# A transformer block in one kernel: token loads of the QKV stages written fifteen steps earlier, and GpSimd's low parts pinned to written order

## The chip, the cores and the metric

The kernel runs on one core of one Trainium2 chip. The metric is the device time of one execution in microseconds (us), as the median of several runs. A profiled execution gives one trace more, and all durations in this text come from such traces.

## What is computed

The reference is a transformer block whose normalised inputs and whose branches are modulated by a condition. There are 2 batch rows of 2048 tokens, 512 features, 16 heads of 32 features and a hidden layer of 2048.

```python
mod = silu(condition) @ Wada + bada
sh_a, sc_a, gt_a, sh_m, sc_m, gt_m = jnp.split(mod, 6, axis=1)
xn = _layernorm(x, g1, be1)
xm = xn * (1.0 + sc_a[:, None, :]) + sh_a[:, None, :]
x = x + gt_a[:, None, :] * _attention(xm, Wqkv, Wproj, bproj)   # causal
xn = _layernorm(x, g2, be2)
xm = xn * (1.0 + sc_m[:, None, :]) + sh_m[:, None, :]
h = gelu(xm @ W1 + b1)
x = x + gt_m[:, None, :] * (h @ W2 + b2)
```

All of it is in float32. The change lies in the part that makes queries, keys and values out of the modulated tokens.

## The kernel before, in words

**Stages.** For batch row 0 and then for row 1 the kernel makes queries, keys and values (the QKV stage) and runs attention. The projection of row 0 stands ahead of row 1's QKV stage, that of row 1 ahead of the MLP, which then runs over all tokens. In the trace the QKV stage of row 0 ends at about 205 us and that of row 1 lies between about 775 and 955 us.

**A QKV stage.** The class `Qkv` (L898) takes a batch row's 2048 tokens in four groups g = 0 to 3 of 512 tokens, that is four tiles of 128 tokens. For each group it runs six units u: units 0 to 3 make the queries and keys of one chunk f of 128 features (four heads), units 4 and 5 the values. A unit (`unit`, L1002) has seven products on half-sized blocks that are summed on three PSUM banks a, b and c, a Strassen-like scheme. Bank a is accumulated on four times and bank b twice; between two of these ScalarE or VectorE copies or adds what the bank holds into an SBUF tile (`first`, `last`, `direct`). The seventh product of a unit is run as third step of the unit after it (`late`, L1197). So a group has 42 steps n, seven a unit, and after each step `tick` (L1145) issues other work of that step. The text writes (g, n) for step n of group g. The first group of a stage has 41 ticks, since no late product precedes its units.

**What a tick does for the next group.** Group g + 1's tokens are loaded at n = 3 (`load_x`, L915, four DMAs of 256 KB on SyncE's queue, into a tile tag `x` with four buffers, so that one group's tokens fill it). Their statistics come at n = 10 to 13 (L218 on VectorE, not pinned), the scaling at n = 15 and 25 (L964 on ScalarE, in place), the transposes on TensorE with the modulation behind them at n = 18 and 28 (`norm`, L970, L214). In row 1's stage the tokens of group 1 are loaded by the projection ahead of it. From n = 7 of group 1 on, each tick also computes some attention scores of the first units of that row (`row.score`): a matmul into one of two banks `s` (L482), and a row maximum of it on VectorE (L498, L504). How many is planned by `count` (L534) from `cum`, a sum of costs by unit (L288: w + 190 for a maximum over w columns, w + 250 where the mask is added): over groups 2 and 3 the plan rises evenly from `cum[0]` to `cum[2]`, and unit 2 comes only when unit 1 is spent.

**High and low parts.** Each result of queries and keys is kept as two tiles: `hi` (L1064, a copy on ScalarE rounded to fp32r) and `lo`, the difference (L1066). For groups 0 and 1 VectorE makes the difference, for groups 2 and 3 GpSimd. Chunk f's queries are split at n = 7f + 5, its keys in the late product at n = 7f + 9. Both tiles are then stored by SyncE (`stored`, L1025, L1031), and the stored heads are read back for the scores (L335, L360) a few ticks after chunk 0's keys. Tiles `hi` have three buffers, tiles `lo` five in row 0 and six in row 1. A unit takes two `lo` tiles, one for queries, one for keys, and both get their first data from bank a and bank b.

**Weight pieces of the MLP.** `Pieces` (L1205) makes sums of blocks of W1 and W2 beside the QKV stages: at a planned tick SyncE loads a piece into idle buffers (L1230, L1239), some ticks later GpSimd begins its sums (L1251), one a tick, or two while more than 12 are waiting, and then stores it (L1267, L1271). A piece in row 0's stage has 4 sums and a store, the last one in row 1's stage 16 sums and a store; that one is loaded at piece tick 74 and begun at tick 80 (L1578).

**What sets the order.** Each engine executes its instructions in the order in which they were put into its queue. The framework chooses that order: it runs the program through a model, and gives each engine at each time the first instruction in written order that the model takes to be ready. An instruction wrapped in `mm` (L204) or `act` (L208) is pinned: it comes behind the instruction written just before it on its engine. All matmuls and the sums of pieces are pinned; DMAs on SyncE, ScalarE's copies, VectorE's statistics and both differences of L1066 aren't.

Of the kernel before, what the change touches and what calls it, by code (L numbers as in the profile page):

```python
# [8 lines left out]
F32 = mybir.dt.float32  # L9
# [3 lines left out]
ALU = mybir.AluOpType  # L13
# [14 lines left out]
def dit_block_kernel(  # L28
# [46 lines left out]
    NG = T // MT  # L75
# [128 lines left out]
    def mm(*args, **kw):  # L204

        return tc.keep_in_program_order(nc.tensor.matmul(*args, **kw))  # L206

    def act(ins):  # L208

        return tc.keep_in_program_order(ins)  # L210
# [687 lines left out]
    class Qkv:  # L898
# [142 lines left out]
        def keys_and_queries(self, g, f, hp):  # L1041

            ops = self.operands(g)
            los = [self.lo_tile(hp) for _ in range(2)]

            def part(i, j):
                return los[i].bitcast(F32)[:, j * HALF_T : (j + 1) * HALF_T]

            def product(ps, n, new):
                for k in range(HK):  # L1050
                    mm(
                        ps, self.w[:, n, k, f * P : (f + 1) * P], ops[n][:, k],
                        start=new and k == 0, stop=k == HK - 1,
                        skip_group_check=not new,
                    )

            def first(ps, i, j):
                scale = HD**-0.5 if i == 0 else 1.0
                nc.scalar.activation(part(i, j), ps, AF.Copy, scale=scale)

            def split(i):
                hi, lo = self.hi_tile(hp), los[i]
                d = lo.bitcast(F32)
                nc.scalar.copy(hi, d)  # L1064
                engine = nc.vector if g < 2 else nc.gpsimd
                engine.tensor_tensor(lo, d, hi.bitcast(F32), ALU.subtract)  # L1066
                self.stored(g, f, i, (hi, lo))

            def last(ps, i, j):
                d = part(i, j)  # L1070
                if i == 0:
                    nc.vector.scalar_tensor_tensor(
                        d, ps, HD**-0.5, d, ALU.mult, ALU.add
                    )
                    if j == 0:
                        split(0)
                else:
                    nc.vector.tensor_tensor(d, d, ps, ALU.add)

            def direct(ps, i, j):  # L1080
                first(ps, i, j)
                split(1)

            return self.unit(product, first, last, direct)
# [53 lines left out]
        def run(self, hp, also, early=()):  # L1138

            row = self.row  # L1140
            late = []
            for g in range(NG):
                at = [0]

                def tick():  # L1145
                    n, at[0] = at[0], at[0] + 1
                    if n >= self.STEPS:
                        return
                    if g + 1 < NG:
                        if n == 3 and g + 1 not in self.xts:  # L1150
                            self.load_x(g + 1)
                        if 10 <= n < 10 + MTT and g + 1 > row.b:
                            self.stats(g + 1, n - 10)
                        if n in (15, 25):
                            self.scaled(g + 1, n // 25)
                        if n in (18, 28):
                            self.norm(g + 1, n // 28)()
                        sums = {36: S1, 38: S2, 40: S3}
                        if n in sums:
                            self.token_sum(g + 1, sums[n])  # L1160
                    elif n == 28:

                        row.rows(0)
                        act(nc.scalar.activation(first, eps, AF.Exp))
                    if g > 0 and n == 2:
                        self.token_sum(g, A22)
                    if n > 9 and self.loads:
                        self.loads.pop(0)()
                    also(g, n)
                    if g > 0 and n >= 7:  # L1170


                        past, of = n - 6, self.STEPS - 7
                        if g == 1:
                            row.score(row.count(cum[0] * past / of, 0))
                        else:
                            past += of * (g - 2)
                            row.score(
                                row.count(
                                    cum[0] + (cum[2] - cum[0]) * past / (2 * of),  # L1180
                                    1 if g == 2 and n < 25 else 2,
                                )
                            )

                for u in range(C + 2):
                    if (g, u) in early:
                        for k, step in enumerate(self.plain(g, u, hp)):
                            step()
                            if k:
                                tick()  # L1190
                        self.token_sum(g, S3)
                        continue
                    if u < C:
                        steps = self.keys_and_queries(g, u, hp)
                    else:
                        steps = self.values(g, u - C)
                    for step in steps[:2] + late + steps[2:6]:  # L1197
                        step()
                        tick()
                    late = steps[6:]  # L1200
            for step in late:
                step()
            assert not self.loads
# [156 lines left out]
    with pool("wada") as wp, pool("qkv0") as qp, pool("hl0") as hp, pool(  # L1360
# [113 lines left out]
        def also(g, n):  # L1474

            if (g, n) == (0, 7):
                for k in range(4):
                    qkv.weight_sum(nc.gpsimd, k, slice(0, P))
            pieces.tick()
            if g == 0 and n == 22:  # L1480
                load_wada(2, 5)
            elif g in (1, 2) and n == 10:
                qkv.columns = modulation(g + 1)
            elif g in (1, 2) and n == 14:
                qkv.columns()
                if g == 1:
                    load_wada(3, 4)
                else:
                    scale_shift(a2, c2, r_g2, r_be2, 3, 4)
# [837 lines left out]
```

## Time and profile before

| | us |
|---|---|
| median of 3 runs | 2258.35 |
| lowest, highest | 2256.87, 2260.15 |
| the profiled execution, device time | 2256.73 |
| its span, first to last instruction | 2255.0 |
| TensorE busy in it | 2211.3 |

The profiled execution's device time is 1.7 us above its span, which is what lies around the instructions. A row of a timeline gives start, duration, engine, line and operation, the written and read tiles, the count, and in brackets the idle time of the engine just before and what ended it. PE is TensorE, DVE VectorE, ACT ScalarE, POOL GpSimd, SPq the queue of SyncE, which issues most DMAs. PEclk is the granted clock of TensorE as a share of full speed. L206 and L214 are lines of helpers, so matmuls and transposes are told apart by their tiles: `ps_xt` are the transposes of tokens, `s` the scores, `ps_a`, `ps_b` and `ps_c` the banks of a unit.

### The profile page before, as it was taken

To read this page: it belongs to the slowest core of one execution; us is meant where nothing else is said; L and a number is where in the kernel's file an instruction comes from. 1 tells how busy PE (TensorE), PEld (TensorE's weight loads), DVE (VectorE), ACT (ScalarE), POOL (GpSimd) and SP (SyncE) were. 2 spreads that over 40 slices of the span, in tenths; PEclk is the share of its full clock that TensorE was granted. 3 is DMA by queue.
4 is the path that set the end of the run, shared out by engine and by line. 5 is a ranking of instruction groups with operands and counts; after the bars stand their busy time and mean duration, and the time that the engine had idled before them with its cause. 6 is when DMAs were issued, how large, how long until landed. Compare 5 with 4: busy or idle time off the path is not lost.

```text
span 2255.0 us, 33464 instructions
## 1 busy us (share of the span) xinstructions
PE 2211.3 (98%) x12057; PEld 1432.2 (64%) x12057; DVE 1535.7 (68%) x3309; ACT 1004.6 (45%) x2012; POOL 1297.9 (58%) x807
## 2 busy tenths in 40 slices
PE   7999999999999999999999999999999999999998
PEld 6777555555543587855555555345787787688687
DVE  4668766777757666777577767663685586576576
ACT  4434555555564244365656555614322422332410
POOL 4253998998983695199989898444205204304210
PEclk9999999999999999999999999999999999999999
DMA  8877143231324799542324113363353354353433
GB/s 281 251 259 193 43 93 75 62 85 48 106 97 135 252 308 313 142 92 62 85 67 104 44 48 131 109 231 129 109 175 133 123 184 145 108 187 126 158 125 110
DMA packets 160510, 311.57 MB, mean 138 GB/s; under 512 B 16544, under 2 KB 48844, under 8 KB 158552
## 3 DMA queue, kind: packets, MB, share of 16 engines
q1 hardware_dynamic: 155488, 285.53, 41.8%
q0 software_dynamic: 4480, 23.36, 2.7%
q8 instruction: 95, 1.56, 0.3%
q14 instruction: 71, 0.58, 0.1%
q10 hardware_dynamic: 376, 0.55, 0.1%
HBM read 229.95 MB, written 87.29 MB: 141 GB/s over the span
## 4 chain that ended last, share of the span: by engine, by line
PE 89%; DVE 4%; DMA 2%; POOL 2%; ACT 1%; issue 1%; SPq 0%; DVEq 0%; ACTq 0%; POOLq 0%
PE ps_a L206 27%; PE st L206 18%; PE ps_b L206 12%; PE o L206 10%; PE s L206 9%; PE ps_c L206 4%; PE ps_o L206 4%; PE sm L206 3%; DVE junk L498 1%; POOL ee L695 1%; PE ps_xt L214 1%; DMA x<-in_x_dram 1%; ACT e L670 1%; DVE mx L504 1%; PE ps_o L214 1%
## 5 line engine op out<-in xcount | busy, mean ns | idle before, releaser
L670 ACT ACTIVATE e<-st 128x512 f32<-128x512 f32 (+1 forms) x1152 | 575.0, 579 | 362.4 <-PE st L206 321.3
L504 DVE TENSOR_REDUCE mx<-s 128x1 f32<-128x512 f32 x576 | 381.9, 686 | 199.0 <-PE s L206 197.9
L695 POOL TENSOR_TENSOR ee<-ee,e 128x2048 f32<-128x2048 f32 x106 | 485.8, 4583 | 10.3 <-ACT e L670 4.3
L206 PE MATMUL st<-qst,kst 128*128 128x512 f32 (+3 forms) x1280 | 408.7, 386 | 0.0
L206 PE MATMUL s<-kst,qst 128*128 128x512 f32 (+3 forms) x1046 | 382.2, 396 | 8.0 <-DVE mx L498 2.7
L206 PE MATMUL ps_a<-sum,w 128*128 128x256 f32 (+1 forms) x1088 | 328.8, 431 | 0.1
L206 PE MATMUL o<-e,vv 128*32 128x512 f32 (+3 forms) x2560 | 293.2, 537 | 0.3 <-POOL e L682 0.3
L206 PEld LDWEIGHTS st<-qst,kst 128*128 128x128 f32 x1280 | 228.5, 188 | 97.3 <-issue 65.7
L498 DVE CUSTOM_DVE_ANT_0 junk<-s,causal 128x128 bf16<-128x128 f32 (+3 forms) x470 | 220.7, 470 | 61.0 <-PE s L206 46.8
L1795 POOL TENSOR_TENSOR sum<-w 128x256 f32<-128x256 f32 x30 | 21.8, 727 | 397.1 <-DMA w<-w1d 203.1
L206 PEld LDWEIGHTS s<-kst,qst 128*128 128x128 f32 x1046 | 195.4, 189 | 72.4 <-DVE mx L504 15.4
L206 PEld LDWEIGHTS ps_a<-sum,w 128*128 128x128 f32 x1088 | 204.5, 190 | 40.1 <-issue 11.4
L695 POOL TENSOR_TENSOR ee<-e 128x2048 f32<-128x2048 f32 x42 | 192.5, 4583 | 43.5 <-ACT e L670 42.5
L206 PEld LDWEIGHTS <-sel 32*128 32x128 bf16 x1152 | 29.5, 91 | 197.0 <-issue 196.1
L2014 ACT ACTIVATE h<-h,cols 128x512 f32<-128x512 f32 x120 | 76.8, 710 | 136.3 <-DVE h L1716 136.3
L504 DVE TENSOR_REDUCE mx<-st 128x1 f32<-128x512 f32 x192 | 131.0, 682 | 0.5
L682 POOL TENSOR_SCALAR_AFFINE_SELECT e<-e 128x512 f32<-128x512 f32 x128 | 83.3, 669 | 67.2 <-ACT e L670 67.2
L206 PE MATMUL st<-fold,sel 32*128 32x512 bf16 (+1 forms) x1152 | 117.3, 372 | 1.2
L206 PEld LDWEIGHTS o<-e,vv 128*32 128x32 f32 x2560 | 59.1, 108 | 92.3 <-issue 72.8
L1716 DVE TENSOR_TENSOR h<-c,ps_b 128x256 f32<-128x256 f32 x90 | 37.9, 421 | 103.5 <-PE ps_b L206 103.0
L1066 POOL TENSOR_TENSOR lo<-lo,hi 128x512 fp32r<-128x512 f32 x32 | 40.7, 1274 | 114.2 <-ACT hi L1064 109.8
L206 PE MATMUL ps_b<-sum,w 128*128 128x256 f32 (+1 forms) x384 | 95.0, 383 | 0.0
(237 smaller groups left out, 3590.7 us busy)
## 6 DMA issues: line engine op xcount, KB each, us to landing
qst<-q SPq DMA_DIRECT2D x128, 256.0 KB
kst<-k SPq DMA_DIRECT2D x128, 256.0 KB
w<-w1d SPq DMA_DIRECT2D x32, 896.0 KB
w<-w2d SPq DMA_DIRECT2D x28, 1024.0 KB
w<-w2d SPq DMA_DIRECT2D x28, 768.0 KB
q<-hi SPq DMA_DIRECT2D x32, 256.0 KB
q<-lo SPq DMA_DIRECT2D x32, 256.0 KB
k<-hi SPq DMA_DIRECT2D x32, 256.0 KB
```

The costliest lines, as they stand in the source:

```text
L206: return tc.keep_in_program_order(nc.tensor.matmul(*args, **kw))
L214: return tc.keep_in_program_order(nc.tensor.transpose(dst, src, ident[:n, :n]))
L498: nc.vector.tensor_tensor_reduce(junk[:, :w], x, causal[:, QB - w :], 1.0, MASKED, ALU.add, ALU.max, m,)
L504: self.vector(nc.vector.tensor_reduce(m, x, axis=AX.X, op=ALU.max))
L670: act(nc.scalar.activation(e4[:, h, :w], sts[h][:, :w], AF.Exp))
L682: nc.gpsimd.affine_select(d, d, pattern=[[0, HC], [1, P]], compare_op=ALU.is_ge, fill=0.0, base=0, channel_multiplier=-1,)
L695: act(nc.gpsimd.tensor_tensor(dst, x, y, ALU.add))
L1066: engine.tensor_tensor(lo, d, hi.bitcast(F32), ALU.subtract)
L1716: act(nc.vector.tensor_tensor(dst, x, y, ALU.add))
L1795: act(engine.tensor_tensor(dst, u, v, op))
L2014: nc.scalar.activation(d[j], d[j], AF.Gelu, bias=col(r_b1 + half * HF + fs[j], 1))
```

## The change

The tokens of group g + 2 are loaded at step 30 of group g, which is two steps behind the transposes that read the four buffers last. The load at step 3 stays for a group that hasn't been loaded: that is group 1 of row 0. And GpSimd's differences are pinned, as the sums of the pieces are.

```diff
@@ -1063,7 +1063,9 @@
                 d = lo.bitcast(F32)
                 nc.scalar.copy(hi, d)
                 engine = nc.vector if g < 2 else nc.gpsimd
-                engine.tensor_tensor(lo, d, hi.bitcast(F32), ALU.subtract)
+                ins = engine.tensor_tensor(lo, d, hi.bitcast(F32), ALU.subtract)
+                if g >= 2:
+                    act(ins)
                 self.stored(g, f, i, (hi, lo))
 
             def last(ps, i, j):
@@ -1146,6 +1148,8 @@
                     n, at[0] = at[0], at[0] + 1
                     if n >= self.STEPS:
                         return
+                    if n == 30 and g + 2 < NG:
+                        self.load_x(g + 2)
                     if g + 1 < NG:
                         if n == 3 and g + 1 not in self.xts:
                             self.load_x(g + 1)
```

## The prediction on record

> **What bounds the kernel now.** I call the QKV stage of batch row 0 stage 0, that of row 1 stage 1, and write (g, n) for step n of token group g. I read the page's busy shares and its chain first.
>
> ```profile
> PE 2211.3 (98%) x12057; PEld 1432.2 (64%) x12057; DVE 1535.7 (68%) x3309; ACT 1004.6 (45%) x2012; POOL 1297.9 (58%) x807
> PE 89%; DVE 4%; DMA 2%; POOL 2%; ACT 1%; issue 1%; SPq 0%; DVEq 0%; ACTq 0%; POOLq 0%
> ```
>
> TensorE is busy for 98% of the span and carries 89% of the chain. Its matmuls stand in written order, so an edit to loads and GpSimd moves the end only by what it adds to or takes from TensorE's holes, or from its clock. The second view is therefore TensorE's timeline over both stages, searched for idle time that a token load can explain.
>
> ```profile
> 78.08 0.33 PE L214 MATMUL ps_xt<-ident,x 128*128 128x128 f32 x1 [1.01 <-ACT x L964]
> 78.79 0.98 PE L214 MATMUL ps_xt<-ident,x 128*128 128x128 f32 x7 [0.38 <-ACT x L964]
> 119.86 0.80 PE L206 MATMUL s<-kst,qst 128*128 128x512 f32 x1 [2.75 <-DVE mx L498]
> 876.68 0.33 PE L214 MATMUL ps_xt<-ident,x 128*128 128x128 f32 x1 [3.79 <-ACT x L964]
> 877.38 1.75 PE L214 MATMUL ps_xt<-ident,x 128*128 128x128 f32 x7 [0.38 <-ACT x L964]
> ```
>
> Two holes are large: 2.75 us in stage 0 at (2,12) and 3.79 + 0.38 = 4.17 us in stage 1 at (2,18). Both belong to the tokens of group 3. The hole at 78 us (1.39 us, tokens of group 2) shows what stays even when tokens are early: the scaling on ScalarE just ahead of the transposes. VectorE's timeline says why the first hole is there.
>
> ```profile
> 115.91 0.69 DVE L218 BATCH_NORM_STATS2 stat<-x 128x6 f32<-128x512 f32 x1 [2.07 <-DMA x<-in_x_dram]
> 118.51 0.69 DVE L218 BATCH_NORM_STATS2 stat<-x 128x6 f32<-128x512 f32 x1 [0.90 <-DMA x<-in_x_dram]
> 119.12 0.67 DVE L498 CUSTOM_DVE_ANT_0 junk<-s,causal 128x512 bf16<-128x512 f32 x1
> ```
>
> The statistics stand in VectorE's queue, wait 2.07 and 0.90 us for tokens, and the row maximum behind them frees TensorE's score bank too late. The holes also cost clock; the stretches show it (after the span come the busy times, then PEclk).
>
> ```profile
> 118.00:122.00 4.00, 2.14 (x6) 1.78 (x6) 2.89 (x7) 0.00 (x0) 0.00 (x0) 0.64 1.02 346
> 122.00:126.00 4.00, 4.00 (x11) 3.12 (x11) 2.90 (x8) 0.82 (x2) 2.37 (x3) 0.51 0.30 112
> 126.00:130.00 4.00, 4.00 (x24) 3.58 (x23) 2.42 (x8) 3.36 (x7) 1.62 (x3) 1.00 0.82 211
> 877.00:880.00 3.00, 2.62 (x11) 2.43 (x11) 0.40 (x1) 2.71 (x6) 2.92 (x3) 0.50 0.94 188
> ```
>
> After the 2.75 us hole the granted clock is about half until 126 us: 2.14 x 0.5 + 4.00 x 0.49 = 3.0 us lost. After the 4.17 us hole it is half for one stretch: 2.62 x 0.5 = 1.3 us.
>
> **The loads.** Nothing is added or removed: in each stage the same four DMAs for groups 2 and 3 are written at (0,30) and (1,30) instead of (1,3) and (2,3). Group 1's loads stay. What counts is what SyncE's queue has between the two places.
>
> ```profile
> 58.57 0.34 SPq L1031 DMA_DIRECT2D k<-lo  x1
> 59.00 1.83 SPq L919 DMA_DIRECT2D x<-in_x_dram  x4
> 107.15 0.32 SPq L1031 DMA_DIRECT2D k<-lo  x1
> 107.57 4.91 SPq L1230 DMA_DIRECT2D kst<-in_L_cond_W_dram  x4
> 112.58 1.84 SPq L919 DMA_DIRECT2D x<-in_x_dram  x4
> 816.80 0.32 SPq L1031 DMA_DIRECT2D k<-lo  x1
> 817.21 1.83 SPq L919 DMA_DIRECT2D x<-in_x_dram  x4
> 860.83 0.32 SPq L1031 DMA_DIRECT2D k<-lo  x1
> 861.25 0.93 SPq L1239 DMA_DIRECT2D vv<-in_L_cond_W_dram  x2
> 865.36 1.84 SPq L919 DMA_DIRECT2D x<-in_x_dram  x4
> ```
>
> For group 2 the load already stands right behind the last key store (k<-lo of chunk 3, itself written at (0,30) just ahead of the new load). There is nothing to pass, in either stage: worth 0. For group 3 it passes the weight pieces of the MLP: four DMAs in stage 0, 112.58 - 107.57 = 5.0 us, and eight in stage 1, 865.36 - 861.25 = 4.1 us. The pieces land later by the 1.84 us that the four token DMAs take, plus the gap, 1.9 us. The token buffers are free in time: the transposes of step 28 read them well before.
>
> **Stage 0's gain.** Tokens 5.0 us earlier land at about 111 to 113.5 us (from 115.9 and 118.5), ahead of the 115.91 - 2.07 = 113.84 at which VectorE turns to them. The hole (2.75) and its clock (3.0) go. What is late next is the scaling, for which I leave the 1.39 us of group 2: -2.75 - 3.0 + 1.39 = **-4.4 us**. Ends: -5.8 if nothing is left, 0 if VectorE's statistics, which aren't pinned, are placed earlier too and meet the tokens as late as now.
>
> **The low parts.** Pinning adds no instruction; it adds order. In stage 0 the trace already has the written order: two sums of a weight piece, the low part of chunk 1, then the rest.
>
> ```profile
> 115.37 1.41 POOL L1251 TENSOR_TENSOR kst<-kst 128x256 f32<-128x256 f32 x2
> 123.55 1.27 POOL L1066 TENSOR_TENSOR lo<-lo,hi 128x512 fp32r<-128x512 f32 x1 [6.78 <-ACT hi L1064]
> ```
>
> The 6.78 us of slack ahead of that low part also hide a piece that lands 1.9 us later: 0. Stage 1 is different. Its last piece has 16 sums, two a tick at first, from piece tick 80, which is (1,39); eleven are written before the query part of chunk 0 (2,5), fifteen before its key part (2,9), all before chunk 1. In the trace three low parts run ahead of the first sum.
>
> ```profile
> 861.62 1.27 POOL L1066 TENSOR_TENSOR lo<-lo,hi 128x512 fp32r<-128x512 f32 x1 [10.80 <-ACT hi L1064]
> 864.18 1.27 POOL L1066 TENSOR_TENSOR lo<-lo,hi 128x512 fp32r<-128x512 f32 x1 [1.30 <-DMA vv<-in_L_cond_W_dram]
> 869.33 1.28 POOL L1251 TENSOR_TENSOR vv<-vv,kst 128x512 f32<-128x512 f32 x1 [0.55 <-DMA kst<-in_L_cond_W_dram]
> 879.51 2.10 POOL L1251 TENSOR_TENSOR kst<-kst 128x256 f32<-128x256 f32 x3
> 882.14 0.74 POOL L1251 TENSOR_TENSOR kst<-kst 128x256 f32<-128x256 f32 x1
> 882.82 1.28 POOL L1251 TENSOR_TENSOR qst<-qst 128x128 f32<-128x128 f32 x3
> ```
>
> With the pin the first sum still waits for weights, now until 869.33 + 1.9 = 871.2. Eleven sums take 879.51 + 2.10 - 869.33 = 12.3 us: 883.5. The query part ends 1.27 later at 884.8, and four more sums (0.74 + 1.28) and the key part (1.27) end at 888.1, against 865.5 now. Behind them wait the stores on SyncE, and the tiles `lo`: six, two a chunk, so chunk 3 takes the two that chunk 0 gives back when its stores have landed. TensorE needs these at (2,24) and (2,25), where it accumulates on banks that ScalarE must first have copied into those tiles.
>
> ```profile
> 884.26 1.89 PE L206 MATMUL ps_a<-t,wqk 128*128 128x256 f32 x8
> 886.22 1.03 PE L206 MATMUL ps_b<-xmT,wqk 128*128 128x256 f32 x4
> 895.76 0.32 SPq L1031 DMA_DIRECT2D q<-hi  x1
> 897.73 0.62 ACT L1064 CAST hi<-lo 128x512 fp32r<-128x512 f32 x1 [2.00 <-DMA q<-hi]
> 883.13 0.38 ACT L1059 ACTIVATE lo<-ps_a 128x256 f32<-128x256 f32 x1 [1.12 <-PE ps_a L206]
> ```
>
> A store gives its tile back 897.73 - 895.76 = 2.0 us after issue; the copy takes 0.38. Key tile back: 888.1 + 0.1 + 2.0 + 0.4 = 890.6, plus about 0.3 for the start of the matmul: 890.9, against 886.22 now: +4.7 us. The 4.17 us hole at (2,18) goes, but it lies ahead of this wait and only lengthens it. The new hole is about 9 us in two pieces; its clock costs between the 1.3 and the 3.0 seen above, and I take 2.2, the middle, since the rows show no hole of that size. **Stage 1: +6.9 us.** Ends: +4.1 if the pieces aren't delayed (4.7 - 1.9 + 1.3), +8.3 with the dear clock and one weight store (0.56) among the sums. Below nothing only if the order isn't what holds TensorE, which is a rival.
>
> On the clock, the Trainium skill (page "TensorE: Matmul & The Clock Gate", section "What's actually happening") says that the array falls to half rate after an idle window of some 3.4 us and comes back after as long a busy one, the window running freely. By it the new hole would cost an estimated 1.7 us and the sum would be lower by 0.5; but the 2.75 us row already fell to 0.51, shorter than the window, so the trace does not bear out the threshold, and the halving agrees.
>
> Other queues: key loads of group 2 (L335) stand behind these stores.
>
> ```profile
> 873.89 1.94 SPq L335 DMA_DIRECT2D kst<-k  x4
> 896.89 1.02 PE L206 MATMUL ps_a<-wv,xmT 128*128 128x256 f32 x4
> ```
>
> They would issue at about 890.5 instead of 873.89, take 1.94 and land some 4 us later, as group 3's tokens did from 114.42 to 118.51: near 897. The scores that read them may begin once unit 1 is spent: 4 x (4 x 702 + 378 + 506 + 634 + 762) = 20352 by the planner's costs, unit 2 4 x 2808 more for its second full block, 51936 for both; 39% of 70 steps from step 7 is (2,34), the row at 896.89, some 902 by then. Hidden, with 5 us to spare.
>
> **Sum.** -4.4 + 6.9 = +2.5 us. The profiled run took 2256.73 us (span 2255.0), 1.6 under the median of 2258.35; 2.5 on the run is 2259.2, on the median **2260.9 us**.
>
> **Rivals.** *The low parts come in time* (the sums start early, or the tiles are given back otherwise): stage 1 keeps its gain, -4.17 - 1.3 + 1.39 = -4.1, with stage 0 -8.5: 2249.9. For it: GpSimd idles 10.80 us before 861.62, room for sums if their weights came earlier. Against it: these weights stand behind a key store at 860.83 and now behind the tokens too. *Slower: the statistics follow the load.* Place: VectorE's queue at (2,10) of stage 0. The framework places them by when it expects the tokens; if they move up by the same 5 us they wait as long, and 0 replaces -4.4: +6.9, 2265.2. It decides from a statistic placed before about 111 us. For it: they are unpinned. Against it: group 2's statistics did not wait, though its load was early.
>
> ```profile
> 70.86 0.69 DVE L218 BATCH_NORM_STATS2 stat<-x 128x6 f32<-128x512 f32 x1
> ```
>
> *The change does nothing:* loads and sums are placed as before: 2258.3. The pin makes this unlikely in stage 1.
>
> **Chances.** Forecast 0.46, own range 2255 to 2266; in time 0.28 (2246 to 2254); slower rival 0.20 (2262 to 2269); nothing 0.06. A difference of 0.2%, 4.5 us, is about what a measurement can tell: faster is below 2253.8, slower above 2262.9. Faster 0.27: the in-time rival but for 0.01. Slower 0.34: 0.16 of the forecast and 0.18 of its rival. Within: 0.30 + 0.01 + 0.02 + 0.06 = 0.39. The range 2248 to 2267 cuts about a tenth at each end.
>
> **What would show it.** Right: SyncE issues group 3's tokens ahead of the weight pieces; no hole near 117 us and PEclk 1.0 there; in stage 1 eleven sums ahead of the first low part of group 2, a hole of TensorE at ps_a and ps_b of chunk 3 released by ScalarE's `lo`, and the hole at the transposes gone or short. Wrong: low parts before the sums, no hole at chunk 3, or group 2's loads moved too.

## The result, and the profile after

| | before | after |
|---|---|---|
| median, us | 2258.35 (13 runs) | 2263.77 (13 runs) |
| lowest, highest | 2253.94, 2261.13 | 2261.49, 2266.49 |
| profiled execution, us | 2256.73 | 2262.9 |

The ratio is 1.0030 (95% interval 1.0022 to 1.0037): the change costs 5.4 us by the medians, 6.8 by the ratio. The forecast was 2260.9, that is +2.5: the right sign, and under half the size. From here on, a gain or cost of a kernel in us is worked out from its ratio unless medians or traces are named. Lines behind L1066 have moved by two, those behind L1148 by four (by two or four in the kernels of the experiments).

TensorE's timeline of the changed kernel, and the one of the kernel before for the rows that the prediction didn't show:

```profile
28.68 1.10 PE L206 MATMUL ps_a<-t,wqk 128*128 128x256 f32 x4 [0.89 <-POOL wqk L944]
115.59 1.92 PE L206 MATMUL ps_mod<-vv,sc 128*32 128x512 f32 x16 [0.80 <-DVE mx L504]
127.70 1.04 PE L214 MATMUL ps_xt<-ident,x 128*128 128x128 f32 x8
771.61 1.13 PE L206 MATMUL ps_a<-t,wqk 128*128 128x256 f32 x4 [0.67 <-ACT lo L1059]
836.46 1.13 PE L206 MATMUL ps_a<-xmT,wqk 128*128 128x256 f32 x4 [1.21 <-ACT lo L1059]
843.97 1.89 PE L206 MATMUL ps_a<-wv,xmT 128*128 128x256 f32 x8
886.02 2.07 PE L206 MATMUL ps_a<-t,wqk 128*128 128x256 f32 x4 [7.25 <-ACT lo L1059]
888.32 1.91 PE L206 MATMUL ps_b<-xmT,wqk 128*128 128x256 f32 x4
900.53 1.03 PE L206 MATMUL ps_a<-wv,xmT 128*128 128x256 f32 x4
903.61 0.47 PE L206 MATMUL s<-kst,qst 128*128 128x512 f32 x1 [2.05 <-DMA qst<-q]
905.01 1.03 PE L206 MATMUL ps_b<-wv,t 128*128 128x256 f32 x4
```

```profile
27.86 1.10 PE L206 MATMUL ps_a<-t,wqk 128*128 128x256 f32 x4 [0.89 <-POOL wqk L944]
131.47 1.04 PE L214 MATMUL ps_xt<-ident,x 128*128 128x128 f32 x8
775.57 1.13 PE L206 MATMUL ps_a<-t,wqk 128*128 128x256 f32 x4 [0.67 <-ACT lo L1059]
846.11 1.89 PE L206 MATMUL ps_a<-wv,xmT 128*128 128x256 f32 x8
899.63 1.03 PE L206 MATMUL ps_b<-wv,t 128*128 128x256 f32 x4
```

In stage 0 the hole of 2.75 us ahead of a score is gone, and one of 0.80 us stands ahead of ps_mod; group 3's transposes come 3.77 us earlier, and stage 1 begins 3.96 us earlier. The holes of 3.79 and 0.38 us at step (2,18) are gone, but a hole of 7.25 us stands ahead of ps_a of chunk 3 and one of 2.05 us ahead of a score. At ps_b<-wv,t behind both, TensorE is 905.01 - 899.63 = 5.38 us late. Stage 1 has lost 3.96 + 5.38 = 9.34 us. Of these, 1.82 lie ahead of the rows that the change was to move: at ps_a<-wv,xmT, shortly before group 2, TensorE is only 846.11 - 843.97 = 2.14 us early, with a hole of 1.21 us at 836.46 that the kernel before hasn't. From there on stage 1 loses 2.14 + 5.38 = 7.52 us.

SyncE's queue shows the loads where the diff puts them, ahead of the weights (L1243, L1234):

```profile
108.69 4.63 SPq L919 DMA_DIRECT2D x<-in_x_dram  x4
113.42 1.92 SPq L1234 DMA_DIRECT2D kst<-in_L_cond_W_dram  x4
859.11 1.82 SPq L919 DMA_DIRECT2D x<-in_x_dram  x4
861.03 0.89 SPq L1243 DMA_DIRECT2D vv<-in_L_cond_W_dram  x2
890.57 1.33 SPq L360 DMA_DIRECT2D qst<-q  x1
```

In stage 0 this brings the tokens less than it seems. The four loads behind the key stores now take 4.63 us to issue, where they took 1.84 behind the weights; the four weight DMAs in that place took 4.91. So the last load is issued by 113.32, only 1.1 us before the 114.42 of the kernel before, and VectorE still waits for tokens:

```profile
114.25 0.69 DVE L218 BATCH_NORM_STATS2 stat<-x 128x6 f32<-128x512 f32 x1 [1.43 <-DMA x<-in_x_dram]
```

The row maximum behind this wait (L504, 114.86) frees the bank for which TensorE has its 0.80 us hole. In all seven traces with the load at step 30 in stage 0, the four loads take 3.84 to 5.11 us to issue and VectorE waits 1.35 to 2.19 us. Why that place in the queue is slow isn't shown; in stage 1 the loads take 1.82.

And GpSimd has taken eleven sums (L1255) ahead of the first low part (L1066) of group 2 in stage 1, fifteen ahead of the second:

```profile
868.11 1.26 POOL L1255 TENSOR_TENSOR vv<-vv,kst 128x512 f32<-128x512 f32 x1 [21.34 <-DMA kst<-in_L_cond_W_dram]
880.36 1.27 POOL L1066 TENSOR_TENSOR lo<-lo,hi 128x512 fp32r<-128x512 f32 x1
883.50 1.26 POOL L1066 TENSOR_TENSOR lo<-lo,hi 128x512 fp32r<-128x512 f32 x1
```

GpSimd idles 21.34 us, the last part of it although a low part could be made (without the order the first one starts at 861.41 after 10.81 us of idling, below): the pinned sum at the head of its queue waits for weights. ScalarE's timeline tells how that reaches TensorE.

```profile
881.66 0.62 ACT L1064 CAST hi<-lo 128x512 fp32r<-128x512 f32 x1 [5.99 <-POOL lo L1066]
884.80 0.62 ACT L1064 CAST hi<-lo 128x512 fp32r<-128x512 f32 x1 [2.52 <-POOL lo L1066]
885.32 0.65 ACT L1059 ACTIVATE lo<-ps_a 128x256 f32<-128x256 f32 x2
887.11 0.38 ACT L1059 ACTIVATE lo<-ps_b 128x256 f32<-128x256 f32 x1 [1.14 <-DMA k<-lo]
```

The copy of bank a that frees TensorE (L1059, 885.32) stands in ScalarE's queue behind two casts (L1064), and these wait for GpSimd: there are three `hi` tiles, and a low part must have been made of one before it can be filled again. The tiles `lo` bind only afterwards, by the 1.14 us at 887.11. The theory for the experiments, A: **eleven sums ahead of the first low part hold the `hi` tiles, these ScalarE's queue, and this TensorE.** Rival B: the weights are late because the tokens now pass them, and the written order adds nothing. Rival C, the prediction's wording: the `lo` tiles are what binds, that is, what the copies wait for last.

### The profile page after: what moved, and what is told of

The parts are those of the page before. It is cut to its first block, busy times and chain, and to the rows that moved or that the text cites. A ratio compares the mean times of both kernels' runs of the same rounds, so it can differ in the third digit from the quotient of the medians.

```text
span 2261.2 us, 33461 instructions
## 1 busy us (share of the span) xinstructions
PE 2213.1 (98%) x12057; PEld 1430.7 (63%) x12057; DVE 1536.2 (68%) x3309; ACT 1003.9 (44%) x2012; POOL 1297.4 (57%) x807
## 4 chain that ended last, share of the span: by engine, by line
PE 58%; POOL 2%; DVE 1%; DMA 1%; SPq 0%; issue 0%; ACT 0%; DVEq 0%; POOLq 0%; ACTq 0%
PE ps_a L206 22%; PE ps_b L206 9%; PE st L206 9%; PE o L206 5%; PE s L206 4%; PE ps_c L206 3%; PE ps_o L206 2%; PE sm L206 2%; PE ps_xt L214 1%; DMA qst<-q 1%; POOL ee L695 1%; PE ps_o L214 1%; DVE junk L498 0%; POOL vv L1255 0%; DVE mx L504 0%
## 5 line engine op out<-in xcount | busy, mean ns | idle before, releaser
L504 DVE TENSOR_REDUCE mx<-s 128x1 f32<-128x512 f32 x576 | 381.4, 685 | 204.7 <-PE s L206 203.7
L504 DVE TENSOR_REDUCE mx<-st 128x1 f32<-128x512 f32 x192 | 130.9, 682 | 0.6
L1066 POOL TENSOR_TENSOR lo<-lo,hi 128x512 fp32r<-128x512 f32 x32 | 40.6, 1273 | 96.9 <-ACT hi L1064 87.4
```

Of the source, the lines that this page charges most:

```text
L504: self.vector(nc.vector.tensor_reduce(m, x, axis=AX.X, op=ALU.max))
L1066: ins = engine.tensor_tensor(lo, d, hi.bitcast(F32), ALU.subtract)
```

## The experiments

Ratios are against the kernel before on the same chip, with 95% intervals.

| kernel | median, us | before there, us | ratio |
|---|---|---|---|
| early tokens alone | 2252.1 | 2256.64 | 0.9975 (0.9963 to 0.9986) |
| written order alone | 2267.09 | 2256.64 | 1.0040 (1.0028 to 1.0053) |
| changed, eight `lo` | 2264.98 | 2256.64 | 1.0032 (1.0020 to 1.0043) |
| changed, five `hi` | 2261.09 | 2256.64 | 1.0015 (1.0001 to 1.0030) |
| early tokens in stage 0 alone | 2257.37 | 2257.64 | 0.9996 (0.9987 to 1.0005) |
| early tokens in stage 1 alone | 2254.0 | 2257.05 | 0.9987 (0.9978 to 0.9996) |
| both, order in stage 0 alone | 2251.73 | 2257.64 | 0.9976 (0.9967 to 0.9985) |
| changed, last piece later | 2252.86 | 2257.64 | 0.9982 (0.9973 to 0.9991) |
| tokens at step 29, no order | 2247.06 | 2257.64 | 0.9963 (0.9950 to 0.9975) |
| tokens at step 29, with order | 2261.64 | 2257.05 | 1.0018 (1.0006 to 1.0030) |

### Early tokens without the order

```diff
-                ins = engine.tensor_tensor(lo, d, hi.bitcast(F32), ALU.subtract)
-                if g >= 2:
-                    act(ins)
+                engine.tensor_tensor(lo, d, hi.bitcast(F32), ALU.subtract)
```

> The changed kernel without the order of GpSimd's low parts: the tokens alone are loaded early. Theory A (the written order puts eleven sums of the last MLP weight piece ahead of the low parts, and that makes the 7.25 us hole of TensorE ahead of ps_a of chunk 3 in stage 1): three low parts stand ahead of the first sum again, the hole goes, and both stages keep what the tokens bring, 4.6 us in stage 0 and some 4 in stage 1: about 2250, 8 to 9 us below the kernel before. Theory B (the weight pieces come late because the tokens pass them, and the order adds nothing): the hole stays within 2 us of its 7.25, and the time stays at about 2262.

GpSimd's timeline of this kernel:

```profile
861.41 1.27 POOL L1066 TENSOR_TENSOR lo<-lo,hi 128x512 fp32r<-128x512 f32 x1 [10.81 <-ACT hi L1064]
868.44 1.27 POOL L1066 TENSOR_TENSOR lo<-lo,hi 128x512 fp32r<-128x512 f32 x1 [3.20 <-ACT hi L1064]
870.53 1.27 POOL L1253 TENSOR_TENSOR vv<-vv,kst 128x512 f32<-128x512 f32 x1 [0.82 <-DMA q<-hi]
```

Three low parts, then the sums; no hole of TensorE between 850 and 895 us is longer than 0.72 us. B falls: the weights stand behind the tokens here as well, the first sum starts at 870.53 (869.33 before), and it costs nothing. The gain is 0.0025, 5.6 us, less than the 8 to 9 expected.

### The order without early tokens

```diff
-                    if n == 30 and g + 2 < NG:
-                        self.load_x(g + 2)
```

> The kernel before with the written order of GpSimd's low parts alone: the tokens stay behind the weight pieces. Theory A: eleven sums stand ahead of the first low part of group 2 in stage 1, a hole of some 5 to 7 us opens ahead of ps_a of chunk 3, less what the weights come earlier (1.9 us), and the 2.75 and 3.79 us holes at the transposes of group 3 stay: some 4 to 8 us above the kernel before, 2262 to 2267. Theory B: no hole at chunk 3, 2258, as before.

ScalarE and TensorE, of the kernel with the order alone:

```profile
880.58 0.62 ACT L1064 CAST hi<-lo 128x512 fp32r<-128x512 f32 x1 [9.90 <-POOL lo L1066]
881.11 0.29 ACT L224 ACTIVATE rstd<-mv,eps 128x4 f32<-128x4 f32 x1
882.11 2.22 ACT L964 ACTIVATE x<-x,shift,rstd 128x512 f32<-128x512 f32 x3 [0.71 <-DVE shift L226]
```

```profile
882.98 0.48 PE L214 MATMUL ps_xt<-ident,x 128*128 128x128 f32 x1 [11.62 <-ACT x L964]
```

It is 9.0 us slower than before, above the 4 to 8 expected, and the hole is not where I looked: with the tokens late, the scaling of group 3 (L964) stands behind the same cast, so TensorE stops at the transposes of step (2,18), for 11.62 us. The mechanism is A's; what it hits first is whatever stands next in ScalarE's queue.

### More tiles

```diff
-            return hp.tile([P, MT], F32R, tag="lo", name="lo", bufs=5 + self.row.b)
+            return hp.tile([P, MT], F32R, tag="lo", name="lo", bufs=5 + 3 * self.row.b)
```

> The changed kernel with eight tiles lo in stage 1 in place of six. The prediction's wording (theory C: chunk 3 waits for the tiles lo that chunk 0 gives back after its stores): the hole of 7.25 us goes, and the time falls by 6 to 8 us to about 2255. Theory A as the trace of the changed kernel has it (the three tiles hi bind first: ScalarE's casts of the key part of chunk 1 and the query part of chunk 2 wait for the low parts at 882 and 885, and the copies of chunk 3's banks stand behind those casts in ScalarE's queue): the hole loses only the 1.14 us by which the lo tile is late after the casts, and the time stays within 2 us of 2262.

```diff
-            return hp.tile([P, MT], F32R, tag="hi", name="hi", bufs=3)
+            return hp.tile([P, MT], F32R, tag="hi", name="hi", bufs=3 + 2 * self.row.b)
```

> The changed kernel with five tiles hi in stage 1 in place of three (lo still six). Theory A: the casts of chunks 1 and 2 no longer wait for GpSimd, so ScalarE comes to the copies of chunk 3's banks in time; the first of them then waits for a tile lo that the query part of chunk 0 gives back after its store, about 881.6 + 0.1 + 2.0 = 883.7 us, in place of 885.3, so the 7.25 us hole loses some 1.6 us at ps_a, and ps_b still waits for the key part's tile until 887: the time falls by 1 to 2 us. Theory C (only the tiles lo bind): the hole is the same, and so is the time, 2262.

TensorE with eight `lo`, then with five `hi`:

```profile
885.86 2.07 PE L206 MATMUL ps_a<-t,wqk 128*128 128x256 f32 x4 [6.98 <-ACT lo L1059]
```

```profile
886.58 1.13 PE L206 MATMUL ps_a<-t,wqk 128*128 128x256 f32 x4 [3.10 <-ACT lo L1059]
889.77 2.08 PE L206 MATMUL ps_b<-xmT,wqk 128*128 128x256 f32 x4 [1.83 <-ACT lo L1059]
```

C falls: two more `lo` tiles leave 6.98 of the 7.25 us and the time at 1.0032. With five `hi` tiles the hole is 3.10 + 1.83 = 4.93 us, and ScalarE's copies there wait for stores of `lo` (1.55 us for q<-lo, 2.81 for k<-lo): these bind second. By the ratios this kernel is 0.0015, 3.4 us, under the changed one, where 1 to 2 were expected, but the two intervals overlap, so the times alone don't show a gain; the traces give 1.2 us (table of stage 1 below). Both enlarged at once was not tried.

### The piece later, with the whole change kept

```diff
-                (room_2, 0, 6), (room_1, 16, 24), (room_2, 47, 56), (room_3, 74, 80),
+                (room_2, 0, 6), (room_1, 16, 24), (room_2, 47, 56), (room_3, 74, 96),
```

> The changed kernel, written order and all, with the last weight piece's sums asked for from tick 80 to 96 in place of 74 to 80, so that the written order itself puts the low parts of chunks 0 and 1 ahead of most of the sums. Theory A (the place of the eleven sums ahead of the low parts is the cause, not the order as such): the 7.25 us hole ahead of ps_a of chunk 3 goes, to under 1.5 us, and the time falls to within 3 us of the kernel without the order, 2250 to 2255. Theory B (the weight pieces are late, or an order written out costs by itself): it stays at 2260 or more.

The load of the piece stays at tick 74; its sums begin at tick 96 in place of 80. GpSimd in this kernel, with the order written out:

```profile
868.41 1.27 POOL L1066 TENSOR_TENSOR lo<-lo,hi 128x512 fp32r<-128x512 f32 x1 [3.18 <-ACT hi L1064]
870.39 1.27 POOL L1255 TENSOR_TENSOR vv<-vv,kst 128x512 f32<-128x512 f32 x1 [0.70 <-DMA q<-hi]
875.56 2.51 POOL L1255 TENSOR_TENSOR vv<-vv 128x512 f32<-128x512 f32 x2
878.02 1.28 POOL L1066 TENSOR_TENSOR lo<-lo,hi 128x512 fp32r<-128x512 f32 x1
```

As A expected: 2252.86 us, three low parts ahead of the sums and a fourth after six of them, no hole ahead of ps_a of chunk 3. So a written order as such has no cost that these runs can tell (0.9982 against 0.9975 without it, with overlapping intervals); the one in the change puts work that can run behind work that still waits.

### One stage at a time

```diff
-                    if n == 30 and g + 2 < NG:
+                    if n == 30 and g + 2 < NG and self.row.b == 0:
```

> Tokens loaded early in stage 0 alone, no written order of the low parts: stage 1 is the kernel before. Theory A and the prediction's step for stage 0: the 2.75 us hole at 115.91 and its slow clock go, and nothing else, so TensorE's transposes of step 18 come 3.8 us (with the launch's offset, 4.6) earlier; stage 1 keeps its 3.79 us hole: 4 to 5 us below the kernel before, about 2252, and 3 to 4 us above the kernel with the early tokens in both stages. If the early tokens of stage 0 bring nothing to the end (given back later): 2257.

```diff
-                    if n == 30 and g + 2 < NG:
+                    if n == 30 and g + 2 < NG and self.row.b == 1:
```

> Tokens loaded early in stage 1 alone, no written order; stage 0 is the kernel before. The two halves should add up to the kernel with both (5.6 us below the kernel before), and the half of stage 0 measured 0.3. If the half clock behind the hole of 2.75 us in stage 0 is paid in some executions only (so that early tokens there bring 1 to 4 us by chance of the execution), stage 1 carries most of the gain, for its hole of 3.79 us is longer: 4 to 5.5 us below the kernel before, 2252 to 2253.5. If the prediction's shares hold (4.4 in stage 0, 4.1 in stage 1) and the half of stage 0 was given back by its own changes of stage 1's placement: 4 us below, and the 2.75 us hole with half a clock behind it in the trace.

```diff
-                if g >= 2:
+                if g >= 2 and self.row.b == 0:
                     act(ins)
```

> The changed kernel with the low parts' written order in stage 0 alone. The prediction's step for stage 0 (the placement already had the written order there, so the order is worth 0) and theory A: as the kernel without the order, within 1 us of 2252, and GpSimd in stage 1 has three low parts ahead of the first sum. If the order costs in stage 0 too, through the weight piece that now lands later: 1 to 3 us more, up to 2255.

(The first two without the order, the third with the tokens early in both stages.) The order in stage 0 is worth nothing, as predicted: 2251.73. Early tokens in stage 1 bring 2.9 us (0.9 to 5.0), early tokens in stage 0 bring 0.9 (-1.1 to 2.9), and not the 4 to 5 that theory and prediction had. The two halves add up to 3.8 us, against 5.6 for both together, which is within what the intervals leave open.

### The kernel before, twice more

> The kernel before once more, for a second trace. If the 3.0 us of half clock behind the hole of 2.75 us in stage 0 belong to the hole, they are there again, with PEclk about 0.6 in 118 to 124 us. If they hang on the execution (the phase of the clock's window), the hole is there and the clock may stay 1.0 or fall at another place, and launch may lose 1.5 to 3 us of clock instead, as in the traces of the kernels with early tokens.

> The kernel before, a third trace, for the same question: whether the half clock behind the hole of stage 0 is there in each execution (3.0 us each time), or only in some.

TensorE in the second trace of before, then in the third (ps_qk are the first products of stage 0, summed on a bank of their own; launch is used below for the time up to the first ps_a<-t,wqk):

```profile
18.18 7.13 PE L206 MATMUL ps_qk<-xmT,wqk 128*128 128x512 f32 x16 [1.78 <-DVE xmT L269]
27.93 1.10 PE L206 MATMUL ps_a<-t,wqk 128*128 128x256 f32 x4 [0.89 <-POOL wqk L944]
119.20 0.79 PE L206 MATMUL s<-kst,qst 128*128 128x512 f32 x1 [2.03 <-DVE mx L498]
129.47 1.04 PE L214 MATMUL ps_xt<-ident,x 128*128 128x128 f32 x8
```

```profile
19.30 10.15 PE L206 MATMUL ps_qk<-xmT,wqk 128*128 128x512 f32 x16 [1.78 <-DVE xmT L269]
32.06 1.10 PE L206 MATMUL ps_a<-t,wqk 128*128 128x256 f32 x4 [0.89 <-POOL wv L949]
122.27 0.50 PE L206 MATMUL s<-kst,qst 128*128 128x512 f32 x1 [0.94 <-DVE mx L498]
131.63 1.04 PE L214 MATMUL ps_xt<-ident,x 128*128 128x128 f32 x8
```

The stretches of the two traces (length, TensorE busy, PEclk, DMA share, GB/s):

```profile
118.00:124.00 6.00, 4.80 (x15) 0.72 0.62 209
```

```profile
118.00:124.00 6.00, 4.83 (x28) 1.00 0.99 326
```

The 2.75 us of the hole and the 3.0 us of clock behind it are not fixed by the kernel: a hole is there each time, but its size and its clock differ from execution to execution. In the third trace the first products ran partly at half clock (10.15 us in place of 7.13) and began 1.12 us later, so that TensorE reached its first ps_a<-t,wqk 4.13 us later than in the second; the hole is then 0.94 us and has no half clock behind it. From that matmul to group 3's transposes:

| tokens in stage 0 | first ps_a<-t,wqk at | from there to the transposes of (2,18), us |
|---|---|---|
| late: before, three traces | 27.86, 27.93, 32.06 | 103.61, 101.54, 99.57 |
| late: order alone; stage 1 alone | 29.56, 30.18 | 100.23, 101.96 |
| at step 30, seven traces | 28.33 to 31.74 | 99.02 to 99.83 |
| at step 29, two traces | 29.72, 30.23 | 98.34, 97.84 |

With tokens at step 30 the way takes 99.0 to 99.8 us in all seven; with late ones 99.6 to 103.6, 101.4 in the mean of five. So early tokens in stage 0 bring some 1.9 us in the mean, between nothing and 4. In the trace with the slowest launch they would hardly have brought anything: what launch lost there, the hole gave back. But that is no rule: with the tokens early in stage 1 alone, launch was 2.3 us behind the first trace and the way still took 101.96, with a hole of 1.89 us and a clock of 0.57 over the four us behind it. Where a timed run stood in this isn't seen.

The same for stage 1, from the row ahead of group 2 (846.11 in the first trace of before) to the one behind the two holes (899.63), without the time before group 2, which varies from 70.1 to 73.7 us:

| stage 1 | way, us |
|---|---|
| before, three traces; early tokens in stage 0 alone | 53.52, 54.03, 53.48; 54.53 |
| tokens at step 30, no order in stage 1, three traces | 50.03 to 50.49 |
| tokens at step 30, order, last piece later | 50.41 |
| tokens at step 30, order: changed; eight `lo`; five `hi` | 61.04; 62.11; 59.82 |
| order, late tokens | 62.22 |
| tokens at step 29: no order; order | 49.12; 59.50 |

Early tokens in stage 1 bring 3.6 us here (53.9 and 50.3 in the means), and the order of the change costs 61.04 - 50.3 = 10.7.

### One step earlier

```diff
-                    if n == 30 and g + 2 < NG:
+                    if n == 29 and g + 2 < NG:
```

> Early tokens without the written order, and one step earlier: at step 29 in place of 30, ahead of the key stores of chunk 3. Theory A: the tokens are already in time with step 30 (0.38 us is left of the 4.17 us hole in stage 1, 0.80 of the 2.75 us in stage 0), so the step earlier gives at most 1 us, and the key stores that it passes come 1.8 us later and cost as much or nothing: within 1.5 us of the kernel with the load at step 30, about 2251 to 2253. If the tokens were still late: 2 us less.

> The changed kernel, written order and all, with the tokens loaded at step 29 in place of 30. Theory A: the cost of the written order doesn't hang on where the tokens are loaded: the hole ahead of ps_a of chunk 3 stays at 6 to 8 us and the time is 9 to 13 us above the same kernel without the order (2247), 2256 to 2260. If the tokens ahead of the weight pieces are what delays the sums (theory B), the weights come as late as now and the time is the changed kernel's, 2263; if the order only costs where tokens and pieces collide, 2250.

Without the order this is the fastest kernel of the study, 0.9963, 8.4 us under before. I had expected a difference of at most 1.5 us from step 30; by the ratio it is 2.9 under the kernel with the order in stage 0 alone (4.7 by the medians), on the same chip, though only five runs stand behind it and the intervals overlap. The expectation took the tokens at step 30 to be in time already, and in stage 0 they weren't: VectorE waited for them in every trace. Here they pass the key stores of chunk 3 as well and take 1.84 us to issue, and the first statistic doesn't wait, as SyncE's and VectorE's timelines of this kernel show,

```profile
108.17 1.84 SPq L919 DMA_DIRECT2D x<-in_x_dram  x4
110.11 1.63 SPq L1031 DMA_DIRECT2D k<-hi  x1
112.39 0.69 DVE L218 BATCH_NORM_STATS2 stat<-x 128x6 f32<-128x512 f32 x1
```

and the last hole of stage 0 (1.06 us ahead of ps_mod with the order in stage 0 alone, 0.80 in the changed kernel) is gone; the way from launch is 1.2 to 1.7 us shorter than the mean of the seven, 99.5. From launch to the end the two traces differ by 2.4 us (2247.6 - 30.23 against 2248.1 - 28.33), near the 2.9 of the ratios. With the order, step 29 has the hole ahead of ps_a again, 6.05 us, and 1.0018, a median of 2261.64 and so over the 2260 expected: the order costs 0.0055 here, as it does at step 30 (1.0030 against 0.9975), some 12.4 us both times.

## Why the prediction was right, and where it was wrong

- **Loads.** Right in order: group 2's stayed where it was, group 3's passed the weight pieces. Wrong in time for stage 0: the prediction gave the four loads 1.84 us wherever they stand, and in their new place they took 4.63.
- **Stage 0, -4.4.** By the two profiled executions right (3.77 us earlier, and launch was 28.68 - 27.86 = 0.82 later: -4.6), in the timed runs not: -0.9 there, -1.9 by the traces. This is the step that failed: "The hole (2.75) and its clock (3.0) go". I took one execution's hole and clock for the kernel's: the five traces with late tokens put the way from launch at 99.6 to 103.6 us, and the one that I worked from is the longest. The step before it, "Tokens 5.0 us earlier", failed too: the last load was issued 1.1 us earlier, VectorE still waited 1.43 us, and 0.80 us of a hole stayed. That the profiled pair fits -4.4 is luck.
- **The low parts in stage 0, 0.** Right (0.9976 with the order there, 0.9975 without).
- **The low parts in stage 1: eleven sums, then the query part, then four sums and the key part.** Right to the instruction. In times counted from the row ahead of group 2 (2.14 earlier) the first sum came at 870.3, where I had put 871.2, and the query part ended at 880.36 + 1.27 + 2.14 = 883.8, put at 884.8.
- **What waits behind them: "the tiles `lo`: six".** Wrong tile. The three `hi` tiles bind first, through ScalarE's queue, the `lo` tiles second: eight `lo` change nothing, five `hi` shorten the hole. The Trainium skill (page "TensorE: Matmul & The Clock Gate", table at its head) gives ScalarE a strict first-in, first-out queue; the rows agree: casts that waited 5.99 and 2.52 us kept back a copy whose bank was full. That the hole nearly had the forecast size with the wrong tile is luck: both kinds of tile come free behind the same low parts, and the copy that needed a `lo` as well waited only 1.14 us more.
- **ps_b +4.7 and clock +2.2.** By the profiled pair, counted as above, ps_b is 888.32 - 886.22 + 2.14 = 4.24 later, and to the row 900.53 (896.89 before), with no hole of 0.4 us between, another 1.54 are lost to the clock: 5.78 in place of 6.9. (The whole loss to the clock was 2.7, last section; the rest of it lies ahead of ps_b.)
- **"Hidden, with 5 us to spare".** Wrong: I worked out the key loads' landing, but the query loads (L360) wait for GpSimd and SyncE too, the first of those above at 890.57, and a score stood 2.05 us for one: 1.74 us more, net, which makes 7.52 for stage 1 in place of 6.9.
- **The sum.** The written order was priced against its own rival: 2260.9 - 2249.9 = 11.0 us. Measured: 12.4, 12.4 and, without early tokens, 9.0; by the way through stage 1, 10.7. So the largest term was about right; what the sum had too large is stage 0's gain: with 0.9 in place of 4.4 it would have been +6.0, against the measured 6.8.
- **The rivals.** That low parts come in time was the changed kernel without its order: 2252.7 by the ratio on 2258.35, in place of 2249.9, for the same reason. Early tokens in stage 1, priced there at 4.1, brought 2.9 alone, 3.6 by the traces. Of the slower rival, that the statistics follow the load, a part came: VectorE turned to the first one at 114.25 - 1.43 = 112.82 us in place of 113.84 and waited again, for less time, and the hole behind it shrank.

## What to carry to other kernels

The size of a hole, and the clock behind it, belong to one execution until more traces show them: price a hole as a distance between two landmarks over several traces. A load that is written earlier is earlier only by what its new place in the queue lets it be: look at how long the loads that stand there now take to issue. Before an instruction is pinned on an engine, look at what stands ahead of it in the written order and whether that can run yet; then follow the wait through every tile that the held instruction has yet to free, and through the in-order queue of the engine that fills it, to whatever stands behind. GpSimd, busy for 57% of the span, did better with the order left to the framework than with one that kept it idle for 21.34 us in place of 10.81.

## What the runs showed of the hardware

The same 16 matmuls (ps_qk) at launch took 7.13, 8.55 to 8.83, or 10.15 to 10.16 us, depending on the execution; in the first trace of before the granted clock is 1.00 through them, in the third it is 0.50 up to about 25.4 us. The Trainium skill (page "TensorE: Matmul & The Clock Gate", section "What's actually happening") says that the clock's window runs freely, so that the slow start varies from run to run; these rows agree. In these traces the half clock behind a hole doesn't grow with the hole. In the changed kernel (hole 7.25 us), with eight `lo` (6.98) and at step 29 with the order (6.05), the stretches in which it ends are:

```profile
890.00:891.00 1.00, 1.00 (x4) 0.50 1.08 401
891.00:892.00 1.00, 1.00 (x6) 0.77 0.91 366
```

```profile
889.00:890.00 1.00, 1.00 (x5) 0.69 1.02 416
```

```profile
891.00:892.00 1.00, 1.00 (x5) 0.50 0.97 381
```

That is 5.4, 3.8 and 6.0 us at half clock from the matmul that ends the hole: losses of 2.7, 1.9 and 3.0 us, the most behind the shortest of the three. The prediction took 2.2. In stage 0 with late tokens the holes of 2.75, 2.03 and 1.89 us had half clock behind them, those of 1.11 and 0.94 none. The Trainium skill (same page and section) has the clock fall after an idle window of some 3.4 us; the first three holes are shorter, so these traces don't bear that threshold out.
